# A layer's MLP in blocks: seven block products for eight, with the hidden values kept in DRAM between the two products

## The chip, the cores and the metric

The kernel runs on one core of one Trainium2 chip. A core has five engines that work side by side, each on its own queue of instructions: TensorE (PE in the profile) multiplies matrices into PSUM, VectorE (DVE) and ScalarE (ACT) work on elements and read PSUM and SBUF, GpSimd (POOL) works on elements in SBUF, and SyncE (SP) issues the DMA transfers between DRAM and SBUF. A matmul consists of a weight load (PEld in the profile), which puts up to 128 x 128 values into TensorE, and of a pass, which streams up to 512 columns through it. The metric is the time of one execution on the device in microseconds (us).

## The reference

Two transformer blocks over x [16 batches, 256 tokens, 512 channels] and a context of the same shape. Block 0 is cross attention with 16 heads and a mask, then a layer norm and an MLP with an exact GELU. Block 1 is causal self attention, cross attention and a ReLU MLP, each followed by a layer norm. The part that changes is block 0's MLP:

```python
x = x + out
h = layer_norm(x, n2_w, n2_b)
h = jax.nn.gelu(h @ fc1_w + fc1_b, approximate=False) @ fc2_w + fc2_b
return x + h
```

where fc1_w is 512 x 2048 and fc2_w 2048 x 512. All of it is float32.

## The kernel before

The batches are taken in eight pairs of 512 tokens (NG = 8; a pair is four token tiles of 128). The residual stream lies in DRAM between five phases: block 0's attention, block 0's MLP, block 1's self attention, its cross attention, its MLP. xd[0] is the stream ahead of block 0's MLP, xd[1] behind it.

A float32 product is taken in three passes (mm3, L259). Each operand is split into h, its leading 12 bits (type float32r, fp32r in the profile), and l, the rest; xh wh + xl wh + xh wl is summed in PSUM. To split a value means one copy that rounds (to h) and one subtraction (to l).

Phase 1 (L554) interleaves attention with the projections. In its tail (last, L741) the MLP's first weight is loaded: Mlp0.load_up (L779) brings fc1_w in 16 pieces of 128 x 512, which the norm's gain n2_w scales on POOL, DVE rounds and POOL subtracts (L184 to L186). What the norm's offset adds to the hidden channels is summed in earlier pairs (fc1_offset, L595). Then front (L785) loads the first pair's residual, norms it and turns it (transposes on TensorE, L281) to [channel, token].

Phase 2, the MLP (Mlp0.run, L827), goes pair by pair and through the 16 chunks of 128 hidden channels. For a chunk, up (L795) makes 4 x 3 passes of 512 columns (the tokens) into a bank of PSUM; ACT takes the GELU of it (L798) and DVE splits that (L136, L137). Two chunks later down (L805) uses the split chunk as weights against fc2_w's rows: 4 token tiles x 3 passes of 512 columns (the channels), which sum over all 16 chunks in four banks. At a pair's end DVE adds the residual (L824) and SP stores it. So the hidden values never leave SBUF, and both weights lie in SBUF split, 64 KB a partition each. fc2_w's pieces are loaded as the first pair runs. The order of TensorE's instructions is the order of the program text; the other engines' queues are ordered by a planner, by readiness in a simulated run and by the order of the text.

Of the kernel before, what the change touches and what calls it, by code (L numbers as in the profile page):

```python
# [10 lines left out]
F32 = mybir.dt.float32  # L11
# [9 lines left out]
P = 128  # L21
B, S, C, H = 16, 256, 512, 16
D = C // H  # 32: a head is one 32-row tile of TensorE
HID = 4 * C
KC = C // P  # 128-wide chunks of the channels; each holds 4 heads
HPC = P // D
NB = 2  # batches at a time
NT = S // P  # token tiles in a batch
G = NB * NT  # token tiles at a time
N = G * P  # tokens at a time  # L30
# [3 lines left out]
NEG = -(2.0**100)  # added to what a softmax leaves out  # L34
BIG = 3.0e38
PASS = 216.0  # what TensorE takes for a pass over 512 columns, and for a transpose, in ns
T_PASS = 109.0
R3 = 3 * D  # rows of a head's stacked operands; row R3 carries a bias by key
# [3 lines left out]
def kernel(ctx: ExitStack, tc: tile.TileContext, a, out):  # L42
    """Block 0 (cross attention, then an exact-GELU MLP) and block 1 (causal self attention, cross
    attention, ReLU MLP, each behind a layer norm), in five phases over all batches, with the
    residual stream in DRAM between them.

    A float32 product x w is taken as xh wh + xl wh + xh wl, where h is a float32 rounded to
    TensorE's 12 significant bits and l = the rest, which those 12 bits hold exactly. Where only 32
    rows are contracted (a head's scores) the three are stacked in one pass."""
# [20 lines left out]
    # For both token tiles: NEG right of the diagonal.  # L70
# [13 lines left out]
    # hmask[p, i, i * 4 + j] = 1 where head j of a chunk owns row p.  # L84
# [15 lines left out]
    cvec = const.tile([P, 4, KC], F32, name="cvec")  # qn_w, qn_b, cn_w, cn_b by channel  # L100
# [10 lines left out]
    def of(name, g):  # L111
        """The rows of pair g of an input [B, S, n]."""
        return rows(a[name][NB * g : NB * (g + 1)].rearrange("b s c -> (b s) c"))

# [4 lines left out]
    def split(src, dst, bias=None, scale=None):  # L119
        """dst[0] = (src + bias or src * scale)'s leading bits, dst[1] = the rest."""  # L120
# [17 lines left out]

    class Weight:
        """A weight [kc * 128, cols], its rows times gain, as (h, l) tiles [128, kc, cols]. With  # L140
        an offset by row also offset @ weight, as a "row" for every partition or as "col"s by
        chunk."""
# [26 lines left out]
        def load(self, ks, x0=0, n=C):  # L169
            """Its columns from x0 on, of row chunks ks."""  # L170
            at = slice(x0, x0 + n)
            for k in ks:
# [9 lines left out]
                elif self.form is None:  # L182
                    by = self.gain[:, k : k + 1]
                    nc.gpsimd.tensor_scalar(raw, raw, by, None, ALU.mult)  # L184
                    nc.vector.tensor_copy(h, raw)
                    nc.gpsimd.tensor_tensor(out=l, in0=raw, in1=h.bitcast(F32), op=ALU.subtract)  # L186
                else:
                    by = self.gain[:, k : k + 1]
                    nc.scalar.activation(h, raw, AF.Identity, scale=by)
                    nc.vector.scalar_tensor_tensor(  # L190
                        l, raw, by, h.bitcast(F32), ALU.mult, ALU.subtract
                    )
        def weigh(self, pool):
            """What sums to offset @ weight, of the chunks loaded last."""
# [17 lines left out]
    def weigh(pool, total, raw, offset):  # L212
        """total (or 0) + raw, each row times its offset."""
# [8 lines left out]
    def sum_cols(b, by_k, first=True):  # L222
        """b[:, c] (+)= the sums of by_k's columns of chunk c."""
# [3 lines left out]
        if first:  # L227
            nc.vector.tensor_copy(b, ps[:, 0:4])
        else:
            nc.vector.tensor_tensor(b, b, ps[:, 0:4], ALU.add)  # L230

# [1 line left out]
    def ln_stats(pool, src):  # L233
        """Mean and reciprocal deviation of a token tile."""
# [24 lines left out]
    def mm3(ps, k, kc, w, x):  # L259
        """ps += w' x for chunk k of kc; w and x are (h, l) pairs of operands."""  # L260
# [10 lines left out]
    # After which chunk's projection each token tile of the next input comes.  # L271
# [5 lines left out]
    def transposed(dst, src, t, tag="mm"):  # L277
        """dst (h, l) [channel, chunk, token] of token tile t from src [token, channel]."""
# [12 lines left out]
    def drain(stream):  # L291
        """A stream's result, traced in one go."""
# [6 lines left out]
    def project_t(w, c, src, tag="mm"):  # L299
        """PSUM [out channel of chunk c, token], a chunk of the contraction at a time."""  # L300
# [13 lines left out]
    def project(w, src, t, tag="mm"):  # L314
        """PSUM [token, out channel] of token tile t."""
# [13 lines left out]
    # Two streams of instructions are traced by turns, so that TensorE has products of the one  # L329
    # while the other waits: attention, and everything else. A stream yields what TensorE takes  # L330
    # for what it traced, None where it needs the other to go first, MARK at a pair's start.
# [27 lines left out]
    class Attention:  # L359
        """A stream over jobs, each a pair of batches. A chunk's queries and keys in one batch  # L360
        (a unit) lie with each head's on rows of its own: queries l, h, h, 1 against keys
        h, h, l, bias."""
# [4 lines left out]
        def __init__(self, pool, scratch, n, biased):  # L367
# [8 lines left out]
            self.later = []  # what has time  # L376
            self.done = 0  # units whose results are traced
# [839 lines left out]
```

## Time and profile before

| | |
|---|---|
| three runs, median | 2850.11 us (2846.05 to 2850.15) |
| profiled execution, span | 2846.8 us |
| block 0's attention | 0 to 735 us |
| block 0's MLP | 735 to 1465 us |
| block 1 | 1465 to 2847 us |

Busy us of the engines in these three stretches (TensorE's passes, weight loads, DVE, ACT, POOL), then the granted clock, the DMA engines' share and GB/s:

```profile
0.00:735.00 735.00, 694.01 (x4567) 544.81 (x4568) 482.35 (x1753) 529.39 (x1552) 231.02 (x282) 0.98 0.61 182
1465.00:2847.00 1382.00, 1321.40 (x8943) 1047.77 (x8941) 1007.27 (x3261) 964.81 (x3097) 459.08 (x453) 0.99 0.56 172
```

A line of a timeline reads: start in us, duration in us, engine, line of the kernel, operation, what it writes <- what it reads, shape, and how many instructions the line merges. A record of a pass or of a DVE operation can be longer than the distance to the next one, since they are pipelined; what an instruction costs on a busy engine is the distance from start to start.

### The profile page before, as it was taken

How to read it: one execution, taken by the hardware profiler on the slowest of the kernel's cores; microseconds unless marked ns; L12 is line 12 of the kernel's file. 1: busy time of each engine (PE TensorE's matmuls, PEld its weight loads, DVE VectorE, ACT ScalarE, POOL GpSimd, SP SyncE). 2: the span in 40 equal slices, each digit the busy share in tenths (PEclk: the TensorE clock that was granted, in tenths of full speed). 3: DMA queues.
4: the chain of work that ended last, by engine and by line, in shares of the span. 5: the costliest groups of instructions: out<-in, count | busy, mean ns of one | idle time of the engine just before them, and what ended most of it. 6: DMA issues, size and time to landing. Idle time of an engine off the chain costs nothing.

```text
span 2846.8 us, 50563 instructions
## 1 busy us (share of the span) xinstructions
PE 2734.5 (96%) x16698; PEld 2180.7 (77%) x16698; DVE 1732.9 (61%) x5445; ACT 1610.9 (57%) x4828; POOL 784.0 (28%) x816
## 2 busy tenths in 40 slices
PE   7999999999999999999999999998999999999998
PEld 5777777777788888888877777776777777777787
DVE  6665667656532233323346777776776677776887
ACT  4877777778311111111127777777777777778632
POOL 6222222115710011100011222224433233234533
PEclk9999999999999999999999999999999999999999
DMA  6665656556310000000046556657665566555321
GB/s 228 182 196 168 181 176 192 180 167 173 109 45 24 7 30 30 30 1 30 30 144 191 181 181 185 185 179 211 206 194 177 177 183 182 172 180 174 97 94 60
DMA packets 274323, 393.71 MB, mean 138 GB/s; under 512 B 35216, under 2 KB 183184, under 8 KB 274064
## 3 DMA queue, kind: packets, MB, share of 16 engines
q1 hardware_dynamic: 274064, 390.48, 44.9%
q8 instruction: 135, 2.21, 0.3%
q14 instruction: 124, 1.02, 0.1%
HBM read 247.22 MB, written 143.13 MB: 137 GB/s over the span
## 4 chain that ended last, share of the span: by engine, by line
PE 74%; DMA 9%; DVE 8%; ACT 4%; issue 2%; SPq 2%; POOL 1%; POOLq 0%; ACTq 0%; DVEq 0%
PE ps_p L262 26%; PE ps_v L262 15%; PE acc L262 12%; PE ps_pt L453 8%; PE ps_z L469 5%; PE ps_s L412 5%; DMA d<-qk 3%; DMA x<-xd 3%; PE ps_t L281 2%; ACT e L437 2%; DVE e L427 1%; PE ps_e L892 1%; ACT pt L456 1%; PE ps_z L954 1%; DVE st L237 1%
## 5 line engine op out<-in xcount | busy, mean ns | idle before, releaser
L437 ACT ACTIVATE e<-e,mn 128x256 f32<-128x256 f32 (+1 forms) x1024 | 487.5, 480 | 97.4 <-DVE mn L427 96.3
L456 ACT COPY pt<-ps_pt 128x512 f32<-128x512 f32 (+1 forms) x768 | 421.3, 553 | 131.6 <-PE ps_pt L453 124.4
L453 PE MATMUL ps_pt<-ident,e 128*128 128x128 f32 x2816 | 440.4, 275 | 6.8 <-ACT pt L456 5.9
L798 ACT ACTIVATE hg<-ps_p,b_fc 128x512 f32<-128x512 f32 x128 | 87.9, 687 | 582.3 <-PE ps_p L262 556.0
L453 PEld LDWEIGHTS ps_pt<-ident,e 128*128 128x128 f32 x2816 | 338.2, 141 | 48.1 <-ACT pt L456 12.7
L412 PE MATMUL ps_s<-stack 97*128 97x256 f32 (+1 forms) x1536 | 334.4, 299 | 37.0 <-ACT e L437 22.2
L412 PEld LDWEIGHTS ps_s<-stack 97*128 97x128 f32 (+1 forms) x1536 | 268.3, 191 | 105.3 <-ACT e L437 40.3
L262 PE MATMUL acc<-fc_w_h,hid 128*128 128x512 f32 x1024 | 337.6, 392 | 0.0
L262 PE MATMUL ps_p<-x_t,fc_w_h 128*128 128x512 f32 x1024 | 317.0, 390 | 0.0
L136 DVE CAST hid<-hg 128x512 fp32r<-128x512 f32 x128 | 59.8, 467 | 389.6 <-ACT hg L798 389.5
L437 ACT ACTIVATE e<-ps_s,mn 128x256 f32<-128x256 f32 x512 | 244.4, 496 | 69.7 <-DVE mn L423 64.4
L963 POOL TENSOR_TENSOR x<-x,zz 128x256 f32<-128x256 f32 x128 | 95.1, 743 | 593.4 <-DVE zz L956 563.9
L427 DVE CUSTOM_DVE_ANT_0 e<-mb,ps_s 128x256 f32<-128x256 bf16 x512 | 192.9, 415 | 81.8 <-PE ps_s L412 78.9
L241 POOL TENSOR_TENSOR rstd<-rstd,nhalf 128x1 f32<-128x1 f32 x192 | 126.4, 666 | 370.8 <-DVE rstd L240 322.9
L262 PEld LDWEIGHTS acc<-fc_w_h,hid 128*128 128x128 f32 x1024 | 192.3, 188 | 42.2
L262 PEld LDWEIGHTS ps_p<-x_t,fc_w_h 128*128 128x128 f32 x1024 | 192.3, 188 | 42.0
L262 PE MATMUL ps_p<-x_t,q_h 128*128 128x512 f32 x640 | 213.9, 415 | 3.2 <-DVE qk L128 3.2
L423 DVE TENSOR_REDUCE mn<-ps_s 128x2 f32<-128x512 f32 x256 | 174.4, 682 | 58.0 <-PE ps_s L412 55.9
L469 PE MATMUL ps_z<-pt,v 128*32 128x256 f32 (+1 forms) x3072 | 203.1, 371 | 4.8 <-DVE rr L635 3.6
L262 PE MATMUL ps_p<-x_t,fc_w_l 128*128 128x512 f32 x512 | 201.2, 393 | 0.0
L262 PE MATMUL acc<-fc_w_l,hid 128*128 128x512 f32 x512 | 200.5, 392 | 0.0
L437 ACT ACTIVATION_READ_ACCUMULATOR e<-e,mn 128x1 f32 x1024 | 197.3, 193 | 0.0
(175 smaller groups left out, 5814.0 us busy)
## 6 DMA issues: line engine op xcount, KB each, us to landing
stack<-d SPq DMA_DIRECT2D x1152, 128.0 KB
d<-qk SPq DMA_DIRECT2D x192, 512.0 KB
x<-xd SPq DMA_DIRECT2D x128, 256.0 KB
xd<-x SPq DMA_DIRECT2D x96, 256.0 KB
wst<-in_fc_w_dram SPq DMA_DIRECT2D x48, 256.0 KB
xin<-in_x_dram SPq DMA_DIRECT2D x32, 256.0 KB
xin<-in_ctx_dram SPq DMA_DIRECT2D x32, 256.0 KB
xr<-in_x_dram SPq DMA_DIRECT2D x32, 256.0 KB
```

What stands on the lines that cost most here:

```text
L136: nc.vector.tensor_copy(dst[0], src)
L241: nc.gpsimd.tensor_tensor(out=rstd[:, 1:2], in0=rstd[:, 0:1], in1=nhalf, op=ALU.pow)
L262: nc.tensor.matmul(ps, w[p], x[q], start=(k == 0 and i == 0), stop=(k == kc - 1 and i == 2))
L412: nc.tensor.matmul(ps[:, t, :], u.st[: self.rows, 0, j, ts(t, P)], u.st[: self.rows, 1, j, :], start=True, stop=True,)
L423: nc.vector.tensor_reduce(mn, ps, AX.X, ALU.min)
L427: nc.vector.tensor_tensor_reduce(out=e[:, at], in0=bias[t], in1=ps[:, t, : job.width[t]], scale=-SC, scalar=BIG, op0=ALU.add, op1=ALU.min, ...
L437: nc.scalar.activation(e[:, at], ps[:, t, :] if bias is None else e[:, at], AF.Exp, bias=mn[:, t : t + 1], scale=-1.0, accum_out=u.rs[:, t ...
L453: nc.tensor.transpose(pp[:, ts(x, P)], e[:, at : at + P], ident)
L456: nc.scalar.copy(pt[:, :n], pp[:, :n])
L469: nc.tensor.matmul(z[ts(j, D), w[0] * P :], job.v[u.i * NT + mc][:, u.c * P + j * D : u.c * P + (j + 1) * D], u.pt[j][:, x0 * P : (x0 + le ...
L798: nc.scalar.activation(hg, ps, AF.Gelu, bias=b_fc1[:, k : k + 1], scale=1.0)
L963: nc.gpsimd.tensor_tensor(out=xv, in0=xv, in1=zz, op=ALU.add)
```

## The change

The two products of the MLP are taken in blocks of two by two. In Strassen's scheme (in Winograd's form) seven products of blocks, of sums and differences of the operands' blocks, replace the eight of the plain product, and sums of the seven results give the four blocks of the product.

On the way up a step takes 512 hidden channels (two weights m of 256) of one pair; the blocks are 256 tokens x 256 channels x 128 hidden channels. Each of the seven products is 2 x 2 x 3 passes of 256 columns; the sums of the results are taken out of PSUM by DVE, with two of the seven products added to a bank that holds another. Products 4 and 3 of a step come between products of the next. On the way down a step takes 256 hidden channels of one pair; a product is 2 x 3 passes of 256 columns, and the seven results sum over the pair's eight steps in seven half-used banks; their sums are taken at the pair's end (end), by DVE and POOL.

A weight of 256 hidden channels is held as its seven operands, split (14 KB a partition, eight of them, 112 KB in all). All pairs go up first, and the GELU's outputs go to DRAM unsplit (1 MB a step), then fc2_w takes fc1_w's place, and all pairs go down, with the hidden values read back, summed in blocks and split. The norm's gain and offset are now applied to the turned input, so that fc1_w isn't scaled and fc1_offset goes. Two of the weights (EARLY) are prepared in phase 1's tail, six as the way up begins; fc2_w's are prepared during the last pair's way up and the first pair's way down. Block 1's pools for its first inputs are those of the MLP.

```diff
-            yield from mlp.load_up()
+            for m in range(mlp.EARLY):
+                mlp.weigh(1, m)
+                yield 12 * PASS
...
             for t in range(G):
-                yield mlp.front(0, t, pool, "xr")
+                yield mlp.turn(0, t, mlp.normal(0, t, pool, "xr"))
+            mlp.sums()
+            for i in range(mlp.NP):
+                mlp.operand_up(i)
...
+    def split_lazy(src, h, l):
+
+        nc.scalar.copy(h, src)
+        nc.vector.tensor_tensor(l, src, h.bitcast(F32), ALU.subtract)
...
+        def differences(self, a21, a22, a11, a12, out):
+
+            s1, s2, s3, s4 = out
+            nc.gpsimd.tensor_tensor(out=s1, in0=a21, in1=a22, op=ALU.add)
+            nc.gpsimd.tensor_tensor(out=s3, in0=a11, in1=a21, op=ALU.subtract)
+            nc.vector.tensor_tensor(s2, s1, a11, ALU.subtract)
+            nc.vector.tensor_tensor(s4, a12, s2, ALU.subtract)
...
+            nc.gpsimd.tensor_tensor(out=t1, in0=b[0][1], in1=b[0][0], op=ALU.subtract)
+            nc.gpsimd.tensor_tensor(out=t3, in0=b[1][1], in1=b[0][1], op=ALU.subtract)
+            nc.vector.tensor_tensor(t2, b[1][1], t1, ALU.subtract)
+            nc.vector.tensor_tensor(t4, b[1][0], t2, ALU.subtract)
+            h, l = self.w[m]
+            for i, x in enumerate((b[0][0], b[1][0], b[1][1])):
+                split_lazy(x, like(h[:, i, :]), like(l[:, i, :]))
+            split_lazy(diff, h[:, 3:, :], l[:, 3:, :])
...
+            if on:
+                self.product_up(n, 1, "mm", True)
+                first = self.flat("p1")
+                nc.scalar.copy(first, self.banks[n, "mm"])
...
+            if after:
+                p1, u2, ho = self.open
+                self.product_up(n - 1, 4, "sc", False)
+                add(ho[:, :, 0, self.W :], p1, self.banks.pop((n - 1, "sc")), ALU.add)
+                self.gelu(n - 1, ho, 0, slice(self.W, N))
+            if on:
+                self.product_up(n, 6, "sc", True)
+                v2 = self.flat("u2")
+                add(v2, first, self.banks[n, "sc"], ALU.add)
...
+                self.product_up(n - 1, 3, "pt", False)
+                add(ho[:, :, 1, : self.W], u2, self.banks.pop((n - 1, "pt")), ALU.add)
...
+            self.product_up(n, 5, "pt", True)
+            between[0]()
+            self.product_up(n, 2, "mm", False)
...
+            self.product_up(n, 7, "sc", False)
+            u3 = self.flat("u3")
+            add(u3, first, self.banks[n, "sc"], ALU.add)
+            add(ho[:, :, 1, self.W :], u3, self.banks[n, "pt"], ALU.add)
...
+            for t in range(2):
+                for j, (p, q) in enumerate(((0, 0), (0, 1), (1, 0))):
+                    nc.tensor.matmul(
+                        ps[:, t, :],
+                        x[p][:, ts(t, P)],
+                        w[q][:, bo, :],
...
+            if i == 6:
+                p1 = self.flat("p1")
+                nc.scalar.copy(p1, p[g, 1])
+                u2 = self.u2 = self.flat("u2")
+                add(u2, p1, p[g, 6], ALU.add)
+                nc.gpsimd.tensor_tensor(out=block(0, 0), in0=block(0, 0), in1=p1, op=ALU.add)
+                nc.gpsimd.tensor_tensor(out=block(0, 1), in0=block(0, 1), in1=u2, op=ALU.add)
+            elif i == 2:
+                add(block(0, 0), block(0, 0), p[g, 2], ALU.add)
+            elif i == 7:
+                add(self.u2, self.u2, p[g, 7], ALU.add)
+                nc.gpsimd.tensor_tensor(out=block(1, 1), in0=block(1, 1), in1=self.u2, op=ALU.add)
+                nc.gpsimd.tensor_tensor(out=block(1, 0), in0=block(1, 0), in1=self.u2, op=ALU.add)
+            elif i == 5:
+                add(block(0, 1), block(0, 1), p[g, 5], ALU.add)
+                add(block(1, 1), block(1, 1), p[g, 5], ALU.add)
...
+            for n in range(total):
+                g, m = divmod(n, self.NM)
+                if n + 2 < total:
+                    self.hidden(n + 2)
+                if n + 1 < total:
+                    self.sums_down(n + 1)
+                    self.operands_down(n + 1)
...
+                if m == 2 and g + 1 < NG:
+                    xs[g + 1] = self.residual(g + 1)
+                for i in (1, 6, 2, 7, 5, 4, 3):
+                    if n or i not in (1, 6):
+                        self.product_down(n, i)
+                    if m == self.NM - 1:
+                        self.end(g, i, xs[g])
```

Here weigh(way, m) loads a weight and makes its operands, normal and turn are front in two parts, sums makes a pair's block sums by differences, operand_up and operands_down split operands (split_lazy) for the two ways, hidden reads a step's GELU outputs back, and residual loads a pair's xd[0] and adds fc2_b on POOL.

## The prediction

> **What bounds the kernel now.** I read the page's head first: TensorE is busy 96% of the span and the clock row beside it stays at 9.
>
> ```profile
> span 2846.8 us, 50563 instructions
> PE 2734.5 (96%) x16698; PEld 2180.7 (77%) x16698; DVE 1732.9 (61%) x5445; ACT 1610.9 (57%) x4828; POOL 784.0 (28%) x816
> ```
>
> That is a mean over stages, so next the busy times by stretch: before, in and behind block 0's MLP (columns: stretch, length, busy us and instructions of each engine, clock, DMA share, GB/s).
>
> ```profile
> 676.00:735.00 59.00, 48.96 (x317) 36.53 (x317) 45.19 (x150) 38.75 (x120) 49.05 (x41) 0.88 0.52 144
> 735.00:1465.00 730.00, 719.08 (x3192) 588.13 (x3191) 243.24 (x432) 116.71 (x180) 93.88 (x83) 1.00 0.09 31
> 1465.00:1500.00 35.00, 29.00 (x126) 22.55 (x125) 24.05 (x71) 10.57 (x18) 13.08 (x17) 0.95 0.92 303
> ```
>
> In the MLP's 730 us every other engine is idle two thirds of the time or more: TensorE alone sets the pace. In the 59 us ahead of it POOL is the busiest engine and TensorE idles 10. Third, the order of time inside the MLP, matmuls and weight loads:
>
> ```profile
> 1001.68 0.19 PEld L262 LDWEIGHTS acc<-fc_w_l,hid 128*128 128x128 f32 x1
> 1001.90 0.39 PE L262 MATMUL acc<-fc_w_l,hid 128*128 128x512 f32 x1
> 1001.91 0.41 PEld L262 LDWEIGHTS acc<-fc_w_h,hid 128*128 128x128 f32 x2
> 1002.13 0.61 PE L262 MATMUL acc<-fc_w_h,hid 128*128 128x512 f32 x2
> ...
> 1002.81 0.61 PE L262 MATMUL acc<-fc_w_h,hid 128*128 128x512 f32 x2
> ...
> 1003.49 0.61 PE L262 MATMUL acc<-fc_w_h,hid 128*128 128x512 f32 x2
> ```
>
> Three passes start every 0.68 us, so a pass over 512 columns costs 0.2275 us (0.226 to 0.230 over the stage), whatever its recorded length; the next load runs beneath it. 3072 x 0.2275 = 699; 120 transposes at 0.109 make 13; 18 us are waits (11 of them at the pairs' boundaries) and the ends.
>
> **TensorE after.** Seven products of blocks for eight, on 256 columns: way up 32 steps x 84 = 2688 passes, way down 64 x 42 = 2688, together 5376 half-length passes for 3072 long ones. The only short passes of this weight width stand in attention:
>
> ```profile
> 2229.58 0.40 PE L412 MATMUL ps_s<-stack 97*128 97x256 f32 x2
> 2229.82 0.60 PE L453 MATMUL ps_pt<-ident,e 128*128 128x128 f32 x4
> ```
>
> Two take 0.24 us: 0.12 each. Bounds: 0.114 (half of 0.2275) and 0.19 (the length of a load's record, if loads should set the pace when every pass is short). I take 0.118, next to the row that is the same instruction but for 97 rows of 128: 634 us, 317 for each way, 65 less than 699. A rule speaks against even this. The Trainium skill, "TensorE: Matmul & The Clock Gate", section "The mechanism" of Part 3, says that a weight load overlaps running matmuls only if it goes to other rows; each pass would then pay load and matmul one after the other, and by the page's 128/1.2 = 107 ns for a load the kernel would grow by an estimated 575 us (5376 x 0.107). The load at 1001.91 above goes to the same rows and starts with the matmul, so the row decides. Transposes stay 128 in all.
>
> **The way up's other engines.** Per step DVE has five sums out of PSUM at 0.61 (0.68 recorded; L864 at 1483.88, 1484.49, 1485.09 starts every 0.61), ACT one copy (0.59) and six GELUs (0.4 to 0.69); per pair come seven splits (ACT copies to h, DVE subtracts for the rest l), four sums of blocks (two on POOL), norms and evictions. DVE: 20 x 0.61 + 9 x 0.61 + about 7 = 25 of a pair's 41 us (336 x 0.118 + 1.7). It is cover enough; the tightest wait is P4 of the step before, which adds to a bank that the sum behind P7 has yet to read, with P1's 12 passes (1.4 us) between. I put 0.2 us a step: 6 (bounds 0 and 20).
>
> **Weights.** load_up's 16 chunks and POOL's 16 x (1.6 + 1.3) = 46 us go from attention's tail, and so do fc1_offset's 16 loads, its 16 one-column matmuls and POOL's 22 us in earlier pairs; at nothing, since TensorE is busy all of the 40 us from 600 on while POOL works 2 of them, and its matmuls are worth 4 us at most (0.245 each). Two weighings (about 4 us each, below), the sums and seven splits come into the tail instead. I return 5 of its 10 idle us (bounds 0 and 10). The other six weighings cost 6 x 4.1 = 25 us of DVE and POOL, beside 3 steps x 6 us of the way up's own DVE work; the last pair of weights is due 30 us in and is done by about 38: 8 lost (bounds 0 and 25, the latter if their 512 KB loads queue on SP or for the three buffers: such a load of half the size took 7.47 us in the chain at 669).
>
> **The way down's other engines** are where I expect the gain to go. Now DVE and POOL meet rarely; where they do:
>
> ```profile
> 736.47 1.51 POOL L181 TENSOR_TENSOR fc_w_l<-wst,fc_w_h 128x512 fp32r<-128x512 f32 x1
> 736.87 1.66 DVE L137 TENSOR_TENSOR hid<-hg,hid 128x512 fp32r<-128x512 f32 x1
> 738.12 6.13 POOL L810 TENSOR_TENSOR x<-x,b_fc 128x512 f32<-128x512 f32 x4
> 738.61 1.34 DVE L136 CAST hid<-hg 128x512 fp32r<-128x512 f32 x1
> 739.99 1.66 DVE L137 TENSOR_TENSOR hid<-hg,hid 128x512 fp32r<-128x512 f32 x1
> ```
>
> L137 alone takes 0.69; beside a POOL operation 1.66, ending 0.69 after 0.14 us before POOL's end. They take turns, one of each in 1.54 us. So POOL keeps DVE off for 1.06 (1.54 less a mean DVE turn of 0.48) to 1.14 (1.28 less 0.14) of its 1.28. DVE operations out of PSUM are not held (L133 keeps its 0.68). For half the width: L963's 0.74 gives 0.52 to 0.60; DVE's 128x256 records 0.42 and the next starts 0.34 later (L427 at 692.09, 692.43, 692.77).
>
> Per pair of batches, eight steps:
> - DVE, two SBUF operands: 8 x (7 splits' rests + 2 sums) x 0.34 = 24.5
> - DVE out of PSUM at the end: 7 x 0.61 = 4.3, free to run beside POOL
> - POOL: 16 sums x 0.52 to 0.60 and 8 additions (4 of the residual's bias, 4 at the end) x 1.06 to 1.14 = 16.8 to 18.7
> - TensorE: 336 x 0.118 = 39.6
>
> What leaves is L136, L810 and L824, which nothing waited long for. DVE and POOL together need 41.3 (smallest, the 4.3 hidden) to 47.5 (largest) against TensorE's 39.6: the pair of them becomes the bound. I take 44.5, the middle, as DVE's end additions wait for POOL's four in order. 8 x 44.5 = 356. ACT (seven copies a step, 0.38 by L478's record) has 5.5 us for 2.7. The reloaded hidden is 512 KB a step, 95 GB/s beside the residual's 47, where other stages move 180; loads run two steps ahead: at nothing, and so is the way up's store of 1 MB a step (106 GB/s). Were that cover gone, each pair's first step would wait for a load of the 7.47 us kind, less the step ahead: 2 us a pair, 16 in all, inside the range.
>
> The way down's weights: one weighing is 2 x 0.6 POOL, 5 x 0.34 and a 1024-wide rest (twice 0.61) on DVE: 4.1. About three fit into the last pair's steps (27 us less 8.5 of sums and 4.3 of the first operands); five fall into the first pair's way down: 20. Way down 376, where TensorE alone would need 317.
>
> A rule of the Trainium skill, "SBUF — State Buffer", section "Who interferes with whom", says the same more harshly: with two SBUF operands DVE and a GpSimd instruction that reads SBUF block each other for the whole instruction. With whole records (72 x 0.42 + 16 x 0.74 + 8 x 1.28 = 52.3) the way down would take 418 + 20 and the kernel some 2900.
>
> **Ends.** front(0) of block 1, wkv's loads and the 6 idle us behind 1465 stay as they are; 3 us for the last sums.
>
> **Sum.** 317 + 14 + 6 + 8 + 356 + 20 + 3 = 724 against 730: 6 less; with the tail's 5, 11 less. The profiled execution is 2846.8 by its span, the runs' median 2850.1, 3.3 above; so 2850.1 - 11 = 2839.
>
> **Rivals.**
> 1. *The port costs nothing*: DVE finds its turns while POOL is quiet. Way down 317 + 18 for the late weights = 335, 41 less: 2798. For it: POOL needs only 20 of 40 us and runs a step ahead. Against it: the turns at 738.
> 2. *Slower: DVE's queue stands still at the pairs' ends.* Its sums P2, P5, P4 and P3 wait for POOL's four additions (4 x 1.28 behind the copy of P1) with the next step's splits queued behind them. 47.5 + 3 per pair: 404 + 20, 48 more than mine: 2887. It decides from 45.9 us a pair on (44.5 + 11/8). For it: both queues are in order. Against it: about 3.5 us of products cover the chain.
> 3. *Short passes don't keep 0.118* when nothing long stands between them. At 0.13 the way up grows 32 us, the way down nothing (336 x 0.13 = 43.7 is under 44.5): 2871. From 0.122 on the gain is gone. For it: the attention rows come two at a time. Against it: they follow each other at 0.12 with weights as wide.
>
> **How the numbers follow.** Mine 0.42, rivals 0.2, 0.23, 0.15. A measurement here tells 0.2% (5.7 us) from nothing. Mine spans 2818 to 2858 by its smaller bounds (0.3 faster, 0.09 same, 0.03 slower); rival 1 is all faster, 2 nearly all slower, 3 slower but for 0.02: faster 0.5, same 0.12, slower 0.38. The range leaves out a tenth at each side: the better half of rival 1 and the top of rival 2, 2796 to 2886.
>
> **What would show it.** Right: in the way down DVE's rests with records far above 0.42 beside POOL, TensorE waiting for them, pairs 44 us apart; passes 0.118 apart in the way up. Wrong: pairs 40 us apart (rival 1), DVE idle on POOL's x (rival 2), passes of 0.13 in the way up (rival 3); or waits in the way up, whose order by hand has the least slack, of over 20 us.

## The result and the profile after

The changed kernel takes 2859.11 us (median of nine runs, 2851.03 to 2866.24), the kernel before beside it 2850.11 us (median of nine runs too, 2836.31 to 2853.08). The ratio is 1.0042, 95% interval 1.0026 to 1.0058: slower by some 12 us by the ratio, 9 by the medians. The forecast was 2839: the measured time lies inside its range (2796 to 2886), but on the other side of the kernel before.

The profiled execution of the changed kernel is the longest of its nine (2866.24), so its stages add up to more than the medians differ by: its span is 17.7 us above the span before. Its head, and the page's group for the way down's first passes (busy us, mean ns | idle us just before, and what ended most of it):

```profile
span 2864.5 us, 57571 instructions
PE 2700.0 (94%) x18970; PEld 2270.2 (79%) x18970; DVE 2087.5 (73%) x6129; ACT 1855.6 (65%) x5504; POOL 894.9 (31%) x960
L991 PE MATMUL down<-w_h,x_t 128*128 128x256 f32 x896 | 187.2, 301 | 55.9 <-DVE x L1032 28.5
```

TensorE does more instructions in less busy time, as the change intends, and half of the idle time that shows at this group is put down to one line of DVE: L1032, a sum of a pair's end.

The stretches of the changed kernel (the end of attention, the way up, the way down, block 1; columns as before):

```profile
676.00:726.00 50.00, 36.24 (x229) 26.21 (x224) 32.65 (x103) 29.82 (x90) 10.45 (x13) 0.80 0.20 61
726.00:1074.00 348.00, 336.07 (x2778) 333.98 (x2777) 237.13 (x461) 183.78 (x376) 60.18 (x65) 0.99 0.38 140
1074.00:1479.00 405.00, 353.03 (x2728) 347.48 (x2728) 356.17 (x655) 177.76 (x475) 206.64 (x209) 0.91 0.40 136
1479.00:2865.00 1386.00, 1325.24 (x8946) 1051.16 (x8945) 1008.30 (x3256) 965.86 (x3098) 456.83 (x445) 0.99 0.55 170
```

The MLP now takes 348 + 405 = 753 us where it took 732. It starts 6.2 us earlier than before (its first pass at 726.0 against 732.2); in the profiled executions below, whose attention is the same, it starts at 721.3 to 728.1. Block 1, whose work is the same, took 1386 here and 1382 before; in the executions below it took 1375 to 1386, so that much of the difference between two profiled executions is not the change's. In the way up TensorE is busy all but 12 of 348 us. In the way down it idles 52 us, and the granted clock is 0.91.

**Passes.** Three of them in the way up, in order of time:

```profile
860.23 0.28 PE L880 MATMUL up_sc<-x_t,w_h 128*128 128x256 f32 x1
860.35 0.28 PE L880 MATMUL up_sc<-c_t,w_h 128*128 128x256 f32 x1
860.47 0.28 PE L880 MATMUL up_sc<-x_t,w_l 128*128 128x256 f32 x1
```

They start 0.12 us apart, which is the median of the way up's 2688 passes, each with a weight load of its own beneath it. A usual step up takes 10.08 us (84 x 0.12), or 10.95 where eight transposes lie in it.

**The way down** falls into steps of exactly 5.04 us (42 x 0.12) inside a pair: there TensorE is the bound and DVE keeps up. Behind the first pair only a pair's first two steps are longer, usually 12.0 and 5.5 us for 10.08: 7.4 us too much. The pairs take 66.1, 48.5, 48.1, 47.7, 47.7, 47.7, 47.7 and 51.7 us (in the last one's last step, 8.6 us, lie transposes of block 1). What TensorE waits for in the way down (total us, times, longest):

```profile
PE down L991 <- DVE x L1032: 28.5, 7, 5.4
PE down L991 <- DVE x_t L142: 12.5, 4, 10.9
PE down L991 <- ACT x_t L141: 9.6, 3, 5.3
PE down L991 <- DVE x L1025: 3.4, 6, 1.2
```

L1032 comes seven times, once at each border of two pairs. One such border, where the next pair starts at 1284.09; DVE's order of time first, then POOL's, then the pass that waited and two of those behind it:

```profile
1285.21 0.67 DVE L1025 TENSOR_TENSOR x<-x,down 128x512 f32<-128x512 f32 x1
...
1286.48 0.68 DVE L1027 TENSOR_TENSOR u<-u,down 128x512 f32<-128x512 f32 x1
1287.08 0.68 DVE L1031 TENSOR_TENSOR x<-x,down 128x512 f32<-128x512 f32 x1
1287.68 1.13 DVE L142 TENSOR_TENSOR c_t<-h,c_t 128x256 fp32r<-128x256 f32 x1
1288.73 1.48 DVE L142 TENSOR_TENSOR c_t<-sums,c_t 128x256 fp32r<-128x256 f32 x1
1290.13 0.68 DVE L1036 TENSOR_TENSOR x<-x,down 128x512 f32<-128x512 f32 x1
1290.73 0.62 DVE L142 TENSOR_TENSOR x_t<-h,x_t 128x256 fp32r<-128x256 f32 x1
1291.27 0.68 DVE L1032 TENSOR_TENSOR x<-x,down 128x512 f32<-128x512 f32 x1
```

```profile
1287.24 1.29 POOL L1028 TENSOR_TENSOR x<-x,u 128x512 f32<-128x512 f32 x1 [2.23 <-DVE u L1027]
1288.49 1.44 POOL L1029 TENSOR_TENSOR x<-x,u 128x512 f32<-128x512 f32 x1
```

```profile
1292.09 0.55 PE L991 MATMUL down<-w_h,x_t 128*128 128x256 f32 x1 [3.84 <-DVE x L1032]
...
1296.07 0.41 PE L991 MATMUL down<-w_h,c_t 128*128 128x256 f32 x1
1296.28 0.41 PE L991 MATMUL down<-w_l,c_t 128*128 128x256 f32 x1
```

Product 5 of the new pair may not start before L1032 has read the old product 5 out of its bank. L1032 adds to the block that POOL's L1028 fills, so it can't come before 1288.5; and then it stands behind two rests (L142, the subtractions that give an operand's l) that share their time with POOL's additions (1.13 and 1.48 us where a rest alone takes 0.41), behind L1036, the sum of product 3, whose bank the new pair needs last, and behind one more rest. It ends at 1291.95 and product 5 starts at 1292.09, 8.0 us behind the pair's start.

**And then the passes are slow.** The stretches around that border:

```profile
1262.00:1284.00 22.00, 22.00 (x186) 22.00 (x185) 20.67 (x45) 12.19 (x34) 9.48 (x11) 1.00 0.37 118
1288.20:1292.00 3.80, 0.05 (x1) 0.00 (x0) 3.80 (x6) 0.00 (x0) 3.39 (x5) 0.77 0.46 148
1292.00:1297.20 5.20, 5.11 (x24) 5.14 (x25) 4.38 (x11) 1.83 (x5) 1.80 (x2) 0.51 0.56 208
1297.20:1320.00 22.80, 22.80 (x192) 22.80 (x192) 19.90 (x35) 10.81 (x31) 12.64 (x12) 1.00 0.42 137
```

Behind the wait of 3.8 us the granted clock is 0.51 for 5.2 us, and the passes start every 0.213 us; then it is 1.00 again. 167 of the way down's 2688 passes are such (they start 0.21 to 0.22 us behind the one before): 167 x (0.213 - 0.120) = 15.5 us.

**The first pair** takes 66.1 us, 22.9 more than its 360 passes (336, and the way up's last 24) need at 0.12. Its third step alone takes 20.5. There POOL and DVE stand so:

```profile
1097.07 11.25 POOL L1004 TENSOR_TENSOR x<-x,b_fc 128x512 f32<-128x512 f32 x8
...
1097.31 1.48 DVE L142 TENSOR_TENSOR x_t<-sums,x_t 128x256 fp32r<-128x256 f32 x1
1098.71 1.48 DVE L792 TENSOR_TENSOR sums<-h,sums 128x256 f32<-128x256 f32 x1
1100.12 1.48 DVE L142 TENSOR_TENSOR c_t<-h,c_t 128x256 fp32r<-128x256 f32 x1
```

Eight additions of the residual's bias (L1004, two pairs' worth) run in a row on POOL, and each DVE operation on SBUF beside them takes 1.48 us.

### The profile page after: what moved, and what is told of

Its sections match the earlier page's. It is cut to its first block, busy times and chain, and to the rows that moved or that the text cites. A ratio compares the mean times of both kernels' runs of the same rounds, so it can differ in the third digit from the quotient of the medians.

```text
span 2864.5 us, 57571 instructions
## 1 busy us (share of the span) xinstructions
PE 2700.0 (94%) x18970; PEld 2270.2 (79%) x18970; DVE 2087.5 (73%) x6129; ACT 1855.6 (65%) x5504; POOL 894.9 (31%) x960
## 4 chain that ended last, share of the span: by engine, by line
PE 70%; DVE 11%; DMA 9%; ACT 5%; issue 3%; SPq 1%; POOL 1%; POOLq 0%; DVEq 0%; ACTq 0%
PE ps_v L259 15%; PE ps_p L259 14%; PE down L991 10%; PE ps_pt L450 8%; PE ps_z L466 5%; PE ps_s L409 5%; PE up_sc L880 4%; PE up_pt L880 3%; DMA d<-qk 3%; PE up_mm L880 3%; ACT e L434 2%; PE ps_t L278 2%; DMA x<-xd 2%; DVE e L424 1%; DVE c_t L142 1%
## 5 line engine op out<-in xcount | busy, mean ns | idle before, releaser
L434 ACT ACTIVATE e<-ps_s,mn 128x256 f32<-128x256 f32 x512 | 244.4, 496 | 65.6 <-DVE mn L420 60.2
L991 PE MATMUL down<-w_h,x_t 128*128 128x256 f32 x896 | 187.2, 301 | 55.9 <-DVE x L1032 28.5
L991 PEld LDWEIGHTS down<-w_h,x_t 128*128 128x128 f32 x896 | 155.4, 207 | 61.2 <-issue 34.2
L424 DVE CUSTOM_DVE_ANT_0 e<-tri,ps_s 128x128 f32<-128x128 f32 (+1 forms) x512 | 158.1, 346 | 50.8 <-PE ps_s L409 46.3
L991 PE MATMUL down<-w_h,c_t 128*128 128x256 f32 x896 | 170.2, 286 | 0.0
L466 PEld LDWEIGHTS ps_z<-pt,v 128*32 128x32 f32 x3072 | 84.4, 110 | 106.9 <-issue 27.5
L259 PE MATMUL ps_v<-v_h,c_t 128*128 128x512 f32 x384 | 158.8, 422 | 0.0
L991 PEld LDWEIGHTS down<-w_h,c_t 128*128 128x128 f32 x896 | 145.3, 196 | 0.0
L141 ACT CAST x_t<-sums 128x256 fp32r<-128x256 f32 (+1 forms) x160 | 67.0, 446 | 106.3 <-PE down L991 50.4
```

What stands on the lines that cost most here:

```text
L259: nc.tensor.matmul(ps, w[p], x[q], start=(k == 0 and i == 0), stop=(k == kc - 1 and i == 2))
L424: nc.vector.tensor_tensor_reduce(out=e[:, at], in0=bias[t], in1=ps[:, t, : job.width[t]], scale=-SC, scalar=BIG, op0=ALU.add, op1=ALU.min, ...
L434: nc.scalar.activation(e[:, at], ps[:, t, :] if bias is None else e[:, at], AF.Exp, bias=mn[:, t : t + 1], scale=-1.0, accum_out=u.rs[:, t ...
L466: nc.tensor.matmul(z[ts(j, D), w[0] * P :], job.v[u.i * NT + mc][:, u.c * P + j * D : u.c * P + (j + 1) * D], u.pt[j][:, x0 * P : (x0 + le ...
L991: nc.tensor.matmul(ps[:, t, :], x[p][:, ts(t, P)], w[q][:, bo, :], start=(m == t == j == 0), stop=(m == self.NM - 1 and j == 2), skip_grou ...
```

## The experiments

The theory: the way down loses its time in one place per pair, where the in-order queue of DVE waits for POOL's four additions while the new pair's products need the banks (the place of rival 2); the wait costs more than its length, as the clock falls behind it. The rival theory: DVE and POOL together are simply too busy (the prediction's own reason), so that any work taken from one and given to the other moves the loss, not the order. A third: short passes are slow by themselves in the way down. Every ratio below is to the kernel before on the same chip.

**1. POOL's additions behind the sums that DVE makes.** DVE adds product 2, 5, 4 and 3 to the residual directly; POOL's additions come after, and u3 has a tile of its own.

```diff
+            def into(t, c, y):
+                nc.gpsimd.tensor_tensor(out=block(t, c), in0=block(t, c), in1=y, op=ALU.add)
+            def sums(t, c):
+                add(block(t, c), block(t, c), p[g, i], ALU.add)
...
             elif i == 2:
-                add(block(0, 0), block(0, 0), p[g, 2], ALU.add)
+                sums(0, 0)
+                into(0, 0, self.p1)
...
             elif i == 5:
-                add(block(0, 1), block(0, 1), p[g, 5], ALU.add)
-                add(block(1, 1), block(1, 1), p[g, 5], ALU.add)
+                sums(0, 1)
+                sums(1, 1)
+                into(1, 1, self.u3)
             elif i == 4:
-                add(block(1, 0), block(1, 0), p[g, 4], ALU.add)
+                sums(1, 0)
+                into(1, 0, self.u3)
             elif i == 3:
-                add(block(0, 1), block(0, 1), p[g, 3], ALU.add)
+                sums(0, 1)
+                into(0, 1, self.u2)
```

> At a pair's end DVE's seven sums go into x and the flat tiles without waiting for POOL; POOL's four additions to x follow them. The number of operations of each engine stays. Theory A (DVE's queue stands still behind sums that wait for POOL's additions): the first step of a pair on the way down falls from 12.0 us to about 7 (5.04 of passes, 2 of DVE's surplus), seven boundaries give back about 35 us, the kernel takes some 2824 us. Theory B (POOL's additions hold DVE off the shared port, whoever waits): as much POOL work at the same time, so the step stays at 11 to 12 and the kernel at 2855 or more. Theory C (DVE simply has 7.3 us of its own work in a 5.04 us step): the step falls to 8.5 to 9, the kernel to about 2835.

Measured: 2839.03 us, ratio 0.9976 (0.9964 to 0.9989). No operation is gone or moved to another engine, only the order is another, and the border's excess falls from 7.4 to 4.4 us (steps of 8.2 and 6.3), the usual pair from 47.7 to 44.7. The order of the queue is thus shown to be worth 3 us a border. The step of 8.2 us lies nearer theory C (8.5 to 9, DVE's own work alone) than A (7); against C speak the steps of experiments 2 and 3, which it put at 12 us or more, and experiment 5's of 6.1, with more work for DVE than here. A wait is left, since rests beside POOL's additions still stand ahead of the sum of product 3, and slow passes are left with it. Two stretches of this kernel at a border:

```profile
1283.20:1285.20 2.00, 0.08 (x1) 0.00 (x0) 2.00 (x3) 0.41 (x1) 1.58 (x2) 1.00 0.45 127
1285.20:1289.00 3.80, 3.76 (x19) 3.79 (x20) 3.80 (x5) 1.52 (x4) 3.80 (x5) 0.56 0.61 209
```

Two idle us are enough here for a clock of 0.56 behind them. They aren't always: the same wait stands at six of this kernel's seven borders (1.95 or 1.96 us), the clock falls behind four of them, and behind the last two it stays, as here:

```profile
1372.70:1374.70 2.00, 0.05 (x2) 0.05 (x1) 2.00 (x3) 0.35 (x1) 1.58 (x2) 1.00 0.53 147
1374.70:1378.50 3.80, 3.80 (x32) 3.80 (x33) 3.80 (x5) 1.53 (x4) 3.80 (x5) 1.00 0.56 203
```

**2. The four additions of a pair's end on DVE.**

```diff
-                nc.gpsimd.tensor_tensor(out=block(0, 0), in0=block(0, 0), in1=p1, op=ALU.add)
-                nc.gpsimd.tensor_tensor(out=block(0, 1), in0=block(0, 1), in1=u2, op=ALU.add)
+                add(block(0, 0), block(0, 0), p1, ALU.add)
+                add(block(0, 1), block(0, 1), u2, ALU.add)
...
-                nc.gpsimd.tensor_tensor(out=block(1, 1), in0=block(1, 1), in1=self.u2, op=ALU.add)
-                nc.gpsimd.tensor_tensor(out=block(1, 0), in0=block(1, 0), in1=self.u2, op=ALU.add)
+                add(block(1, 1), block(1, 1), self.u2, ALU.add)
+                add(block(1, 0), block(1, 0), self.u2, ALU.add)
```

> The four additions to x at a pair's end are made by DVE in place of POOL. Theory A: no wait for another queue, but four more operations of 0.61 us on DVE: the boundary step falls from 12.0 to about 9.5, the kernel to about 2840. Theory B: the port is free of POOL's 4 x 1.1 us: about 9, the kernel about 2836. Theory C: DVE's work in that step grows from 7.3 to 9.8 us, so the step stays at 12 or grows, the kernel 2859 or more.

Measured: 2849.92 us, ratio 1.0014 (1.0002 to 1.0027). The border's first step is 10.3 to 10.5 us, the pairs 45.5 and 46.6 in turn, between what the theories said. POOL has no addition left here for DVE to wait for, and still TensorE waits for the same sum as long in all as in the changed kernel:

```profile
PE down L991 <- DVE x L1032: 28.5, 7, 7.1
```

At a usual border that is 3.5 us for 3.84. L1032 now stands behind DVE's own additions, where DVE has no time to spare. So it is the place in DVE's queue that counts, more than whose additions stand ahead of it: moving them to the other engine gives less than moving them in the order.

**3. The way down's sums of blocks on DVE.**

```diff
-        def differences(self, a21, a22, a11, a12, out):
+        def differences(self, a21, a22, a11, a12, out, on=None):
...
-            nc.gpsimd.tensor_tensor(out=s1, in0=a21, in1=a22, op=ALU.add)
-            nc.gpsimd.tensor_tensor(out=s3, in0=a11, in1=a21, op=ALU.subtract)
+            on = on or nc.gpsimd
+            on.tensor_tensor(out=s1, in0=a21, in1=a22, op=ALU.add)
+            on.tensor_tensor(out=s3, in0=a11, in1=a21, op=ALU.subtract)
...
-            self.differences(b[1][0], b[1][1], b[0][0], b[0][1], s)
+            self.differences(b[1][0], b[1][1], b[0][0], b[0][1], s, nc.vector)
```

> The two block sums that POOL makes in every step of both... only of the way down go to DVE; POOL's additions at the pairs' ends stay. Theory A: the chain through POOL stays, a little shorter since no sums queue ahead of its additions: boundary step 10 to 12, kernel 2845 to 2860; the steps in a pair's middle stay at 5.04 (DVE 11 x 0.34 = 3.7). Theory B: two holds of 0.55 us less a step: boundary about 9, kernel about 2835. Theory C: DVE has 0.7 us more in every step: boundary 12.5 to 13, kernel about 2865.

Measured: 2843.74 us, ratio 0.9989 (0.9977 to 1.0001). Sixteen sums a pair leave POOL, so the two engines meet much more rarely, but the border keeps its wait:

```profile
PE down L992 <- DVE x L1033: 27.7, 7, 5.3
```

27.7 us for 28.5 (the line is one further on): how often DVE and POOL meet inside a pair is not what makes this wait. It does cost something: the border's first step is 10.3 to 10.8 us, as the short waits for L1025 and L1027 (3.4 and 1.9 us in the changed kernel) are gone, the first pair is 60.2, and the kernel takes 0.5% less than the changed one (by the two ratios). So the rival theory has a part of the loss; at the borders the order has the larger one (3 us of the 7.4, against 1.2 to 2.1 here).

**4. Passes that fill the wait.** 24 passes whose result nobody reads, behind product 7 of each pair's first step from the second pair on.

```diff
+        def fill(self, n):
+            ps, x = bank("z", "fill"), self.down_slots(n, 0)
+            for j in range(24):
+                nc.tensor.matmul(
+                    ps[:, : self.W], x[0][:, :P], self.w[0][0][:, 0, :], start=True, stop=True
+                )
...
                         self.product_down(n, i)
+                    if m == 0 and g and i in (7,):
+                        self.fill(n)
```

> Where TensorE waits in the first step of a pair (behind product 7) 24 passes into a bank that nothing reads are put in, 2.9 us. If the passes of 0.21 us behind each wait come from TensorE's clock having been lowered by the wait, they go back to 0.12: 24 x 0.09 = 2.2 us a boundary, 16 us in all, kernel about 2844. If they come from operands that are late, nothing changes, or the fill delays: 2859 to 2865.

Measured: 2841.56 us, ratio 0.9982 (0.9968 to 0.9997): 2.9 us of useless passes at seven borders make the kernel faster by 0.6% (the two ratios, 1.0042 and 0.9982), about 17 us, than it is without them. The way down from the second pair on, in the changed kernel and then in this one:

```profile
1130.00:1450.00 320.00, 286.18 (x2224) 282.73 (x2223) 287.93 (x523) 140.95 (x382) 168.77 (x164) 0.93 0.41 137
```

```profile
1130.00:1467.00 337.00, 322.36 (x2644) 317.96 (x2643) 304.00 (x579) 149.16 (x414) 175.98 (x180) 1.00 0.43 144
```

The clock is 1.00 instead of 0.93, and the slow passes, counted as above, fall from 167 to 31, all of them in the first pair. So the third theory falls: the short passes of the way down run at 0.12 where no idle time stands ahead of them. The usual pairs take 44.9 to 46.3 us.

**5. Both: all four additions behind the last sum, the sums of blocks on DVE.** Experiment 1 with the four `into` lines moved behind the sum of product 3, and experiment 3.

```diff
             elif i == 3:
                 sums(0, 1)
+                into(0, 0, self.p1)
+                into(0, 1, self.u2)
+                into(1, 0, self.u3)
+                into(1, 1, self.u3)
```

> POOL's four additions at a pair's end come behind the last of DVE's sums, and the steps' block sums are all on DVE, so that POOL has nothing to do beside a boundary's DVE work. If wait and port together made the boundary's 7.4 us, little but DVE's own surplus stays: 7 x 0.61 + 11 x 0.34 = 8.0 us against 5.04, less what it is ahead (some 1.3 a step): first step of a pair 6.5 to 7.5, pair 42 to 43 (47.7 as changed, 44.7 and 46 with either part alone), kernel about 2822, a ratio to the kernel before of 0.991. If DVE's own work is what counts, the pair stays at 44.7 or more and the kernel at 2838.

Measured: 2819.06 us, ratio 0.9915 (0.9899 to 0.9931). A border's first step is 6.1 us, 1.1 above its passes, and the usual pair 42.7. One step further on another loss now shows: the step in the middle pairs that has the residual's four additions is 6.1 to 6.5 instead of 5.04 us, and 11.1 in the second pair.

**6. The residual asked for later.** Experiment 5, with the first residual traced in the first pair's fourth step and the second in its seventh.

```diff
-            xs = {0: self.residual(0)}
+            xs = {}
...
-                if m == 2 and g + 1 < NG:
+                if m == 3 and g == 0:
+                    xs[0] = self.residual(0)
+                if m == (6 if g == 0 else 2) and g + 1 < NG:
                     xs[g + 1] = self.residual(g + 1)
```

> As e5, and the bias additions of the first two pairs' residuals (eight on POOL, together 11 us in a row in the first pair's third step) come at the fourth and seventh step, four each. If they hold DVE off the port there, as every DVE record of 1.48 us beside one of POOL's 1.44 says, the first pair (66 us as changed) falls by 8 to 10 us and the kernel to some 2813. If the second weights alone make the first pair long, it stays at 60 to 66.

Measured: 2814.8 us, ratio 0.9903 (0.9873 to 0.9933), not to be told from experiment 5. The planner drew the eight additions together all the same, between 1096 and 1113 us, in the third to the fifth step of the first pair, which still takes 60.9 us. The edit did not do what it should, so it tells nothing of the additions' price.

**7. No late weights.** fc1's first two weights stand for all eight on both ways, and neither fc1's other six nor fc2's are prepared; that part of the computation is left out.

```diff
-                w = [y[:, bo, :].rearrange("p (k c) -> p k c", k=2) for y in self.w[2 * s + mm]]
+                w = [y[:, bo, :].rearrange("p (k c) -> p k c", k=2) for y in self.w[mm]]
...
-            ps, x, w = self.banks[g, i], self.down_slots(n, ao), self.w[m]
+            ps, x, w = self.banks[g, i], self.down_slots(n, ao), self.w[m % 2]
...
-            for m in range(self.EARLY, self.NM):
-                self.weigh(1, m)
...
-                if g == NG - 1 and s >= 1:
-                    for m in (2 * s - 2, 2 * s - 1):
-                        self.weigh(2, m)
...
-            self.weigh(2, self.NM - 2)
-            self.weigh(2, self.NM - 1)
```

> As changed, but of fc1's weights only the two made in attention's tail are made and stand for all eight, and none of fc2's is made (the way down uses fc1's two): what the weights cost is left out, the passes stay. The way up's first four steps as changed take 50.1 us where 42.0 is the later pairs' time: 42 is expected, 8 less. The first pair's way down takes 66 us: if the weights made it long, 47.7 without them, 18 less, together 26 less and a kernel of about 2833; if the residual's eight POOL additions did, it stays above 56.

Measured: 2837.63 us, ratio 0.9971 (0.9957 to 0.9985). The way up's first pair falls from 50.1 to 42.0 us (8.1), its last pair, up to the first pass of the way down, from 44.7 to 37.4 (7.3), the way down's first pair from 66.1 to 58.6 (7.5). The first pair was expected to lose 18; it keeps 15.4 us above its passes: 6.3 in its first step and 9.1 in its fifth. For the fifth, POOL and then DVE:

```profile
1082.31 8.39 POOL L1004 TENSOR_TENSOR x<-x,b_fc 128x512 f32<-128x512 f32 x6
1090.67 0.72 POOL L789 TENSOR_TENSOR sums<-h 128x256 f32<-128x256 f32 x1
```

```profile
1091.42 0.93 DVE L791 TENSOR_TENSOR sums<-sums,h 128x256 f32<-128x256 f32 x1 [3.05 <-POOL sums L789]
```

The next step's sums of blocks (L789) stand behind the residual's additions in POOL's queue; DVE idles 3.05 us for them, and TensorE 5.5 for what follows.

**8. The residual's additions on DVE too.** Experiment 5 and this:

```diff
-                nc.gpsimd.tensor_tensor(
-                    out=x[:, t, :], in0=x[:, t, :], in1=self.b_fc2, op=ALU.add
-                )
+                nc.vector.tensor_tensor(x[:, t, :], x[:, t, :], self.b_fc2, ALU.add)
```

> As e5, and the residual's bias additions are made by DVE: 4 x 0.61 us a pair more for DVE, nothing on POOL but the four additions at a pair's end. In e6 POOL still made the first two pairs' eight additions in a row (the planner drew them together), each DVE operation beside one taking 1.4 to 1.5 us. If the port is what made the first pair's fifth step 11.5 us, that step falls to 5 to 7, the first pair to about 53, the kernel to some 2808. If the second weights' DVE work fills the first pair anyway, it stays at 60 and DVE's additions lengthen the others: 2820.

Measured: 2806.54 us, ratio 0.9852 (0.9832 to 0.9872): faster than both kernels, 43 us below the one before. The pairs are 57.0, 41.3, 43.2, 41.3, 42.1, 41.3, 41.3 and 44.8 us for passes of 40.3; the way down takes 351 us for 405. Its stretch, and what TensorE waits for from the second pair on:

```profile
1073.00:1424.00 351.00, 334.83 (x2716) 331.55 (x2717) 329.06 (x813) 178.92 (x475) 73.47 (x46) 0.98 0.47 156
```

```profile
PE down L992 <- DVE x L1020: 6.8, 8, 1.9
PE down L992 <- DVE x_t L142: 0.6, 1, 0.6
```

DVE does 158 operations more than in the changed kernel's way down and is busy 27 us less (329 for 356): here an operation of POOL on SBUF takes DVE more time than doing that work itself.

**9. The weights' differences on DVE as well** (the two lines of weigh that are POOL's, on top of experiment 8).

```diff
-            nc.gpsimd.tensor_tensor(out=t1, in0=b[0][1], in1=b[0][0], op=ALU.subtract)
-            nc.gpsimd.tensor_tensor(out=t3, in0=b[1][1], in1=b[0][1], op=ALU.subtract)
+            nc.vector.tensor_tensor(t1, b[0][1], b[0][0], ALU.subtract)
+            nc.vector.tensor_tensor(t3, b[1][1], b[0][1], ALU.subtract)
```

> As e8, and the differences of the weights' blocks are made by DVE too, in both ways. If POOL's hold counts there as well, the way up's first four steps (50.1 us as changed, 42.0 without late weights) fall by 2 to 4 us and the first pair's way down by as much: 2 to 8 us less than e8. If DVE's own work counts (2 x 0.34 more for each of twelve weights), they grow by 2 to 4 each.

Measured: 2810.74 us, ratio 0.9871 (0.9854 to 0.9888), so no better; the way down's first pair is 58.7 us for 57.0. It fits a first pair that waits for DVE's own work, but 1.7 us between two executions don't show it.

**10. The residual's additions on DVE alone**, the edit of experiment 8 in the changed kernel.

> The changed kernel with one edit: the residual's bias additions (eight in a row for the first two pairs, then four a pair) on DVE instead of POOL. If the row of eight on POOL is what makes the first pair's third step 20.5 us, that step falls to 10 to 14 us (eight times 0.61 of DVE come in its place), the first pair from 66.1 to 57 to 60, the other pairs stay at 47.7 as their four additions lie in the pair's middle: 6 to 9 us less, about 2851. If the step is long because of the late weights alone, the first pair stays at 64 to 68 and the time at 2859.

Measured: 2845.26 us, ratio 1.0002 (0.9989 to 1.0015). The third step falls from 20.5 to 17.6 us only, the first pair to 63.3: the row of additions is gone from POOL and stands, mixed with the rests, in DVE's queue, ahead of the rests that the step's second product waits for (7.1 us). So the row seems to cost by where it stands, on either engine. The borders' first steps fell as well, from 12.0 to 10.7 to 11.0 us from the third pair on: the wait for the sum of product 5 (two lines further up) is as long as before, but those for L1025 and L1027 are gone here too.

```profile
PE down L991 <- DVE x L1030: 28.5, 7, 5.5
```

Why DVE is that much earlier there stays open.

**11. Experiment 8 without the late weights**, with the same part of the computation left out as in experiment 7.

> The kernel with the pairs' end sums and the way down's additions moved (block sums and residual on DVE, the four additions at the end of the pair behind all of DVE's seven) without the weights from the third on, so part of the computation is left out: fc1's first two stand for all eight on both ways. If late weights and the residual's row of additions are all that the first pair lacks, its way up falls from 50 to 42 us and its way down from 57 to 44 to 48: 17 to 21 less than with the weights, about 2787. If the first pair waits for something else (its first operands, loads of hidden values), its way down stays above 52 and the time above 2795.

Measured: 2789.8 us (two runs), ratio 0.9807 (0.9781 to 0.9833). The way up's first pair is 42.1 us as expected, the way down's first pair 54.5 and not 44 to 48: late weights and the row of additions are not all. Its first step takes 15.8 us for 7.9, as the way down's first operands come late; its first waits, and the stretch that follows them:

```profile
1060.73 0.39 PE L992 MATMUL down<-w_h,x_t 128*128 128x256 f32 x1 [2.89 <-ACT x_t L141]
1062.64 0.79 PE L992 MATMUL down<-w_h,x_t 128*128 128x256 f32 x2 [1.41 <-DVE x_t L142]
```

```profile
1060.80:1071.00 10.20, 8.79 (x49) 8.59 (x50) 7.11 (x21) 4.17 (x10) 0.00 (x0) 0.67 0.45 165
```

Over the stretch with these 4.3 us of waits the clock is 0.67. Another 3.5 us go in the fifth step.

## Why the prediction was wrong, point by point

- *The tail of attention, 5 us back*: 6.2 in the two profiled executions. Right, as far as a start that lies between 721.3 and 728.1 in the others can tell.
- *A pass 0.118*: 0.120, the value of the attention row itself; over 5376 passes that is 11 us, as much as the whole gain forecast, though by the prediction's own sum only the way up's half counts, as a pair down was put at 44.5 whatever a pass takes. The number taken should have been the row's. Rival 3's figure of 0.122, at which the gain is gone, was nearly reached. That a weight load runs beneath a pass on the same rows is confirmed for all of the way up: 334 us of loads in 348.
- *The way up, 345*: 348. Eight for late weights is right to the tenth (8.1, experiment 7). The six us of waits were looked for in the steps; there are none, each usual step is 10.08 or 10.95. Instead some 7 us are lost at the end, where the last pair's way up prepares fc2's weights and the way down's first operands queue behind them.
- *The weights of the way down, 20 us in the first pair*: 7.5 there and the 7.3 just told. That the first pair came out near its forecast (66.1 for 64.5) was luck: without the weights (experiment 7) it still lost 9.1 us in the step of the residual's additions and 6.3 with late first operands, and neither is in the sum.
- *8 x 44.5 = 356, "the pair of them becomes the bound"*: this is the step that failed. It added up the time of DVE and POOL over a pair and shared it out evenly; that DVE's end additions wait in order was its reason for the middle of a range of busy times, and the wait got no length of its own. Measured, DVE and POOL are no bound in 46 of the 63 steps whose length can be read, which take TensorE's 5.04; behind the first pair all is lost in one place per pair. In the other steps TensorE is the bound, so the time that DVE has left there doesn't make the wait good: 7.4 us a border, made of the wait for L1032 and of slow passes behind it. The usual pair is 47.7, and the seven pairs behind the first take 339 us for the 314 (7 x 44.5 + 3) forecast. The kernel turned from faster to slower here: rival 2 names the place, the two queues and the point of decision (45.9 a pair), and put the pair at 50.5. It is right on the place and half right on the cause, as the wait for L1032 is as long without POOL's additions (experiment 2). Against it the prediction held that 3.5 us of products cover the chain; the chain ends 8.0 us behind the pair's start.
- *The port*: turns are taken as forecast (a rest beside an addition takes 1.48 us), but they cost only where someone waits. The Trainium skill, "SBUF — State Buffer", section "Who interferes with whom", says that the two block each other for the whole instruction. The records agree that they hold each other up (1.48 for 0.41), but for somewhat less than the whole instruction: one of each starts every 1.41 us (eight additions in 11.25), where by the prediction's figures a lone addition of 1.28 and a rest of 0.34 would come to 1.62. Added up over a pair the rule would have made the kernel some 2900; it measured 2859.
- *Not thought of*: the slow passes, 15.5 us in the way down, which the sum doesn't have. With the borders' waits filled, the changed kernel is faster than the one before (experiment 4: 0.9982).
- *Signs that were named*: passes 0.12 apart and long DVE records came; pairs 44 us apart did not; "DVE idle on POOL's x" (rival 2's sign) shows as DVE's rests ahead of L1032, not as idle time.

## What to carry to other kernels

A busy sum over a stage tells whether an engine can keep up, not whether it does: look for the one step in which an in-order queue holds a result that the next step's products need a bank for, and price that chain from its first instruction to its last. Where a queue is in order, put the operations that free a bank ahead of those that only finish a result, and do not put two-operand work on GpSimd beside VectorE's if VectorE can do it in less than it is held up for (experiment 8). A wait of a few us on TensorE should be priced with the half-speed passes that can follow it (about 2 us a border here).

## What the runs showed of the hardware that was not expected

Behind an idle time of 2.0 us (experiment 1) and of 3.8 us (the changed kernel) the granted clock was 0.56 and 0.51 over the next 3.8 and 5.2 us, and passes of 256 columns started every 0.213 instead of 0.120 us. In experiment 1 the same wait had this behind it at four borders of six; what decides it, no run here shows. Filling the idle time with passes that nobody reads kept the clock at 1.00 and made the kernel faster (experiment 4). The Trainium skill, "TensorE: Matmul & The Clock Gate", Part 1, gives an idle window of about 3.4 us for the clock's fall to half; here 2.0 us were followed by it at those four borders, so a shorter wait can be enough.
